# Attention's sums taken two steps at a time, the neighbour mask as a product, and other edits to a two-layer image kernel

## The chip, the cores and the metric

The kernel runs on one core of one Trainium2 chip. Its time is device microseconds of that core. Before the change three runs gave a median of 8884.31 us (8876.86 to 8887.73).

A core has five engines with instruction queues of their own: PE (matrix products; its weight loads are shown as PEld), DVE (vector), ACT (activations and copies), POOL (a second, general vector engine) and SP (used here to issue DMA transfers). Each runs its own queue in order, and they meet only by semaphores.

## The reference

x is two images of 96 channels and 96x96 pixels, float32. Two layers follow each other; each adds a mixing block and then a feed-forward block (FFN).

```python
# layer 0: normalization over channels, then
xz = in_proj(x); xin, z = split(xz)                   # 192 channels each
offset = tanh(conv1x1(gelu(bn(conv3x3(xin)))))        # where to sample
xs = grid_sample(xin, ref + offset)
# 16x16 sub-grids of 36 pixels, 4 directions, 16 states:
h = h * exp(dt * A) + dt * u * B;  y = C . h + D * u  # dt = softplus(dt_w . r + dt_b)
x = x + out_proj(layernorm(sum of 4 directions) * silu(z))
# layer 1: normalization over channels, then
k, v = kv_w . xn;  samp = mean of 2x2 pixels of xn;  q = q_w . samp
attn = softmax over the 9216 keys of (k^T q / sqrt(32))    # 3 heads of 32, 2304 queries
dist = v . attn                                            # 96 x 48 x 48
dmat = softmax over 3x3 neighbours of (xn . samp / sqrt(96))
feature = dmat . (3x3 neighbours of dist)
x = x + proj_w . (feature + depthwise5x5(v) + lepe_b) + proj_b
# both layers: x = x + FFN(normalization(x)), 96 -> 384 -> 96, relu,
# factors rounded to an 8-bit format (5 exponent, 2 mantissa bits), sums to a 16-bit one
```

## The kernel before, in words

**The plan.** Layer 0, and the two outer stages of layer 1, are written as lists of operations, each with an engine, a cost and a due time (`_Plan.op`). `_Plan.order` simulates the engines and their buffers with these costs and takes, engine by engine, the operation that can start first, the due time breaking ties. The order it finds is then held per engine, SP among them. So a changed cost or buffer can move any instruction of the same plan.

**Start.** `_l0_weights` loads layer 0's weights, nearly all on SP's queue, and brings some into other layouts: dt_b (the scan's bias) comes in pieces by 24 tiny loads; A_logs goes by 16 loads into the DRAM tensor `ad` with other strides (L381), is read back as `at` by four loads (L387) and is transposed on PE; `Ds` follows (L400). After these stands the first load of an image's stripe, `xt` (L464).

**Layer 0** (`_layer0`) is one plan over 32 stripes of 576 pixels: a front part (projection, offsets, sampling), the recurrence (`h`, L1045 on DVE and L1050 on POOL), and a back part with the FFN, which writes the result to the DRAM tensor `x2d`. Its buffers lie in four pools, made in the order front, hand, rep, back; the weights' temporaries had the same memory before them.

**Layer 1** (`_layer1`) first loads its weights, builds the neighbour mask (`_l1_mask`) and the FFN's weights, and then does for each image:

1. *Before* (`_l1_before`), a plan over 16 stripes of 576 pixels: load `nxt` from x2d (L1138), normalize (`nxc`, `nva`) into `xn`, which stays in SBUF for the whole image, project `k` (kH) and `v` (vT), pool 2x2 pixels on POOL (xs), project the queries (qH).
2. *Attention* (`_l1_attention`). A bound on the scores is computed and read into a register as a flag; it chooses between a shifted softmax and the plain one, `_l1_packed`, which is what runs. The queries are taken in chunks of 10 rows of 48 (480), the last of 8 rows. A head has 32 channels, so three heads fill three of PE's four row strips; the fourth does in turn a quarter of each head's keys (`SHARED` = 18 blocks of 128). A chunk so has 54 steps in place of 72. A step has four score products of 32 rows (L1382), two exponentials of 960 into `pr` (L1386), four `av` products with the values (L1443), and one DVE addition of all four strips, 1920 elements, into `sums` (L1456), from which the softmax's denominators come. When the fourth strip has done a head, `sums` of it is added to that head's (L1458). PE's order is held: the scores of step j+1 stand before the av products of step j. A chunk ends with `close`, whose parts are run within the next chunk: copy `av` out, products with ones over `sums`, reciprocal on DVE (step 2), products that join the strips, and `dist` = product of both on DVE (step 6).
3. *Rows* (`_l1_rows`), a plan over 8 row blocks of 12 rows: values of the block into `vch` with two edge columns (L1550); per group of 384 pixels the scores with two rows of pooled cells (`st`, L1574), exponential (`e`, L1578), multiplication by the 0/1 mask on POOL (L1580), sums and products with `dist` (`pd`, `po`), feature `ft`; the 25 taps of the depthwise convolution, 20 on DVE as multiply-and-add of 1152 elements (L1612, L1615), five on PE as products with `pt`, the projection scaled by the tap's weight (L1631); the projection of `ft` and of `acc`; then the FFN and the store.

Of the kernel before, what the change touches and what calls it, by code (L numbers as in the profile page):

```python
# [101 lines left out]
class _Plan:  # L102
# [3 lines left out]
    def __init__(self, k):  # L106
        self.k, self.ops, self.slots, self.queues = k, [], {}, {}

# [9 lines left out]
    def op(self, eng, cost, run, r=(), w=(), due=0.0, tab=None, also=()):  # L118
        o = _Op(eng, cost, run, due, tab)
        ref = lambda t: t if isinstance(t, tuple) else (t, None)  # L120
        meets = lambda a, b: a is None or b is None or a == b
        for t, key in map(ref, r):
            o.deps.update(p for p, q in t.writes if meets(key, q))
        for t, key in map(ref, w):
            o.deps.update(p for p, q in t.writes + t.reads if meets(key, q))
        for t, key in map(ref, r):
            t.reads.append((o, key))
        for t, key in map(ref, w):
            t.writes.append((o, key))
        o.deps.discard(o)  # L130
        for t in [x[0] for x in map(ref, list(r) + list(w))] + list(also):
            if t not in o.tiles:
                o.tiles.append(t)
        for t in o.tiles:
            if not t.users and t.tag != "p":
                t.queue.append(t)
            t.users.append(o)
        self.ops.append(o)
        return o
# [127 lines left out]
def _l0_weights(k, a, cp, tmp, ps, dram):  # L267
# [51 lines left out]
    for kg in range(KG):  # L319
        o, kk = kg % 2, kg // 2  # L320
        nc.vector.tensor_copy(k.w_dl[:, :, o, kk * 6 : kk * 6 + 6], xp[:, :, kg, 0:6])
        rows = slice(kk * 6, kk * 6 + 6)
        nc.sync.dma_start(dt_w[rows, o, kk, :], a["dt_w"][kg, :, 0:128])
        nc.sync.dma_start(dt_w[rows, o, 2, kk * 64 : kk * 64 + 64], a["dt_w"][kg, :, 128:])
        b = a["dt_b"]
        for blk in range(2 * NBL):
            half, r = divmod(blk, NBL)
            src = b[r * CB : r * CB + CB, kg, half : half + 1]
            if blk < 4:
                nc.sync.dma_start(k.dt_b[blk::4, o, kk : kk + 1], src)  # L330
            else:
                r0 = kk * 64 + blk - 4
                nc.sync.dma_start(k.dt_b[r0 : kk * 64 + 64 : 2, o, 2:3], src)
        for j in range(4):
            src = xp[:, :, kg, 6 + NS :] if j == 1 else xp[:, :, kg, 6 : 6 + NS]
            nc.vector.tensor_copy(k.w_bc[:, :, o, j, kk, :], src)

# [42 lines left out]
    for n in range(NS):  # L380
        nc.sync.dma_start(ad[n].rearrange("k (d g) -> d k g", g=NG), src[n])  # L381
# [4 lines left out]
    for i in range(NQ):  # L386
        nc.sync.dma_start(  # L387
            at0[i * na : (i + 1) * na], rows[i]
        )
# [10 lines left out]
    nc.sync.dma_start(ds4, a["Ds"])  # L400
# [678 lines left out]
def _layer0(k, tc, a, x, x2d):  # L1079
# [3 lines left out]
    with ExitStack() as st:  # L1083
# [9 lines left out]
        P.front, P.hand, P.rep, P.back = (pool(n, 1) for n in ("front", "hand", "rep", "back"))  # L1093
# [20 lines left out]
        front(0)  # L1114
        for n in range(len(stripes)):
            front(n + 1)
            _l0_scan(k, P, S, n, F[n], tau)
            back(n)
# [7 lines left out]
def _l1_before(k, P, S, W, M, x2d):  # L1126
# [7 lines left out]
    xn, xs, kH, qH, vT, mk, mq = map(held, ("xn", "xs", "kH", "qH", "vT", "mk", "mq"))  # L1134

    def stripe(s):
# [24 lines left out]
        for c in range(2):  # L1161
            norm(c)
        for n, f in enumerate((ALU.max, ALU.min)):
            op("dve", T, lambda n=n, f=f: nc.vector.tensor_reduce(
                mk.ap[:, n, s : s + 1], kH.ap[:C, s * T : (s + 1) * T], AX.X, f),
                ((kH, s),), ((mk, (n, s)),))
# [187 lines left out]
def _l1_packed(k, tc, wk, ps, pa, M):  # L1354
# [3 lines left out]

    nc = k.nc
# [6 lines left out]
    q3 = {}  # L1366
# [7 lines left out]
    def scores(m, j):  # L1374
        n, (p, t) = chunks[m][1] * CELLS, divmod(j, SHARED)
        pr = wk.tile([128, 4, 480], F32, tag="pr", name="pr", bufs=3)
        two = [ps.tile([128, 2, 512], F32, tag="s", name="sc", bufs=3) for _ in range(2)]
        for s in range(4):
            rows = slice(s * HD, (s + 1) * HD)
            k0 = (SHARED + j) * 128 if s < HEADS else (p * SHARED + t) * 128  # L1380
            q = qH[rows, cells(m)] if s < HEADS else q3[m, p][rows, :n]
            nc.tensor.matmul(  # L1382
                two[s // 2][:, s % 2, :n], kH[rows, k0 : k0 + 128], q, start=True, stop=True
            )
        for i in range(2):
            nc.scalar.activation(  # L1386
                pr[:, 2 * i : 2 * i + 2, :n], two[i][:, :, :n], AF.Exp, scale=HD**-0.5
            )
        return pr

    def close(m, av, sums, av3):

        n = chunks[m][1] * CELLS
        avs = wk.tile([128, 480], F32, tag="avs", name="avs", bufs=2)
# [3 lines left out]
        for hd in range(HEADS):  # L1398
            nc.tensor.matmul(
                av[hd * HD : (hd + 1) * HD, :n], k.ones[:, :HD], sums[:, hd, :n],  # L1400
                start=True, stop=True,
            )
# [24 lines left out]
    for m in range(len(chunks)):  # L1427
        n = chunks[m][1] * CELLS
        sums = wk.tile([128, 4, 480], F32, tag="sums", name="sums", bufs=2)
        av3 = wk.tile([128, 2, 480], F32, tag="av3", name="av3", bufs=2)  # L1430
        for j in range(steps):
# [7 lines left out]
            for s in range(4):  # L1439
# [6 lines left out]
                    pr[:, s, :n],  # L1446
# [3 lines left out]
            if j == 0:  # L1450
                nc.vector.tensor_copy(sums[:, :, :n], pr[:, :, :n])
            elif t == 0:
                nc.vector.tensor_tensor(sums[:, :3, :n], sums[:, :3, :n], pr[:, :3, :n], ALU.add)
                nc.vector.tensor_copy(sums[:, 3, :n], pr[:, 3, :n])
            else:
                nc.vector.tensor_tensor(sums[:, :, :n], sums[:, :, :n], pr[:, :, :n], ALU.add)  # L1456
            if t == SHARED - 1:
                nc.vector.tensor_tensor(sums[:, p, :n], sums[:, p, :n], sums[:, 3, :n], ALU.add)  # L1458
                if p < 2:
                    nc.scalar.copy(av3[last, p, :n], other[last, :n])  # L1460
# [3 lines left out]
            if rest and j in (2, 6):  # L1464
                next(rest)
# [52 lines left out]
ON_PE = tuple(range(5))  # L1518


def _l1_rows(k, P, S, W, ffn, M, distT, x2, out, q, at):
# [8 lines left out]
    xn, xs = S.held(M.xn, "xn"), S.held(M.xs, "xs")  # L1530
# [3 lines left out]
    y0 = q * R - 2  # L1534

# [10 lines left out]
    def values(g):  # L1546
# [4 lines left out]
            pv.ap[:C, :n], W.v, xn.ap[:, lo * HW : hi * HW], start=True, stop=True),  # L1551
# [13 lines left out]
    def near(i):  # L1565
        j = 3 * q + i
        toks = slice(j * 384, (j + 1) * 384)
        e = [S.tile(P.wk, [NEAR, 384], "e", 4) for _ in range(2)]
        po, pd, rd = ps("po"), ps("pd"), S.tile(P.wk, [C, 384], "rd", 2)
        for t in range(2):  # L1570
            st = ps("st")

            def part(t=t, st=st):
                op("pe", 384, lambda: nc.tensor.matmul(  # L1574
                    st.ap[:NEAR, :384],
                    xs.ap[:, 2 * j + 2 * t : 2 * j + 2 * t + 2, :].rearrange("p r w -> p (r w)"),
                    xn.ap[:, toks], start=True, stop=True), (xs, xn), (st,), (e[t],))
                op("act", 384, lambda: nc.scalar.activation(  # L1578
                    e[t].ap, st.ap[:NEAR, :384], AF.Exp, scale=C**-0.5), (st,), (e[t],), tab="e")
                op("pool", 384, lambda: nc.gpsimd.tensor_tensor(  # L1580
                    e[t].ap, e[t].ap, W.mask[:, t], ALU.mult), (), (e[t],))
# [26 lines left out]
    for n, t in enumerate(t for t in range(25) if t not in ON_PE):  # L1608
        def tap(n=n, t=t):
# [4 lines left out]
            else:  # L1614
                S.op("dve", 1.6, lambda: nc.vector.scalar_tensor_tensor(  # L1615
# [70 lines left out]
def _l1_mask(k, cp):  # L1686
# [14 lines left out]
    mask = cp.tile([NEAR, 2, 384], F32, tag="mask", name="mask")  # L1701
    m = mask.rearrange("p t (i r w s) -> p t i r w s", i=2, r=2, s=2)
    for t in range(2):
        for i in range(2):
            src = both if t == i else band[:, 1 - t]
            for r in range(2):
                nc.vector.tensor_copy(
                    m[:, t, i, r], src.unsqueeze(2).to_broadcast([NEAR, CELLS, 2])
                )
    return mask  # L1710


def _layer1(k, tc, a, x2d, out):
    nc = k.nc
    with ExitStack() as st:
# [3 lines left out]

        def load(name, shape):  # L1720
            t = cp.tile(shape, F32, tag=name, name=name)
            nc.sync.dma_start(t, a[name])
            return t

        W.k, W.v = load("k_w", [C, C]), load("v_w", [C, C])
        W.q, W.p = load("q_w", [C, C]), load("proj_w", [C, C])
        W.pb, W.lw = load("proj_b", [C, 1]), load("lepe_w", [C, 25])
        W.mask = _l1_mask(k, cp)

        W.pt = cp.tile([C, len(ON_PE), C], F32, tag="pt", name="pt")  # L1730
        for n, t in enumerate(ON_PE):
            nc.vector.tensor_scalar(W.pt[:, n], W.p, W.lw[:, t : t + 1], None, ALU.mult)
        with tc.tile_pool(name="l1t", bufs=1) as tmp, tc.tile_pool(name="l1p", bufs=1, space=PSUM) as ps:
            ffn = _ffn_weights(k, cp, tmp, "f1", a["W1_1"], a["b1_1"], a["W2_1"], a["b2_1"])
            lb = tmp.tile([C, 1], F32, tag="lb", name="lb")
            nc.sync.dma_start(lb, a["lepe_b"])
            pl = ps.tile([128, 512], F32, tag="pl", name="pl")
            nc.tensor.matmul(pl[:C, 0:1], W.p, lb, start=True, stop=True)
            nc.vector.tensor_tensor(W.pb, W.pb, pl[:C, 0:1], ALU.add)
        img = pool("img", 1)  # L1740

        def plan(st, work):
# [3 lines left out]
            S = _Plan(k)  # L1746
            start = len(nc.cur_bb.bb.instructions)
# [4 lines left out]
        for b in range(NB):  # L1752
            M = Ctx()
            M.xn = img.tile([C, NTOK], F32, tag="xn", name="xn")
# [3 lines left out]
            nc.gpsimd.memset(M.dist, 0.0)  # L1758
            with tc.tile_pool(name="kqv", bufs=1) as kqv:
# [5 lines left out]
                with ExitStack() as st:  # L1765
                    plan(st, lambda P, S: _l1_before(k, P, S, W, M, x2d[b]))
                _l1_attention(k, tc, M)
# [13 lines left out]
def tile_metaformer(ctx: ExitStack, tc: tile.TileContext, a, out):  # L1781
# [11 lines left out]

    k.mean96 = filled("mean96", [C, C], 1.0 / C)
# [86 lines left out]
```

## Time and profile before

| what | us |
|---|---|
| median of three runs | 8884.31 |
| the profiled execution | 8876.68 |
| its span, first to last instruction | 8874.9 |
| mean granted PE clock | 0.893 |
| start, before the recurrence | 175.5 |
| layer 0's recurrence | 6565.6 |
| change of layers | 45.5 |
| image 0: before, attention, rows | 78.2, 623.4, 340.8 |
| image 1: before, attention, rows | 81.9, 624.4, 339.6 |

The shares over the whole span are PE 84%, DVE 91%, ACT 72%, POOL 70%; since layer 0 has three quarters of the span, they are mostly layer 0's. The stretches were cut where the first or last instruction of a stage stands in the trace. In the change of layers (6741.1 to 6786.6) PE is busy for 25.7 us and DVE for 7.5.

### The profile page before, as it was taken

The page shows a single profiled execution, that of the slowest core. Times are in us where ns is not written, and L with a number is a line of the kernel's source. Part 1 is how long each engine was busy: PE and PEld are TensorE (multiplying, and loading weights), DVE is VectorE, ACT ScalarE, POOL GpSimd, SP SyncE. Part 2 cuts the span into 40 slices and gives each one's busy share as a digit, 9 for nine tenths or more (in the row PEclk, how much of TensorE's full clock was granted, in tenths as well). Part 3 has the DMA queues.
Part 4 walks back from the last instruction along what each step waited for, and adds up shares of the span by engine and source line. Part 5 has one row for each costly group of instructions (what it writes and reads, how often), then busy time and mean ns, then how long its engine had stood idle before and what let it go on. Part 6 is the DMA issues. An engine that isn't in the chain of part 4 may idle for free. (4 is left out here: it accounts for less than half of the span.)

```text
span 8874.9 us, 120352 instructions
## 1 busy us (share of the span) xinstructions
PE 7426.3 (84%) x43537; PEld 3500.8 (39%) x43537; DVE 8093.4 (91%) x5663; ACT 6381.7 (72%) x10720; POOL 6189.7 (70%) x3931
## 2 busy tenths in 40 slices
PE   6788888888788888888888888888856999989998
PEld 3333334444343344434444433443423333543345
DVE  2999999999999999999999999999996998969988
ACT  4677777777777777777777777777754876677766
POOL 3999999988999889899898889898974001310022
PEclk9899889999988888889898988888956999999999
DMA  2444444444444444444444444444441000010000
GB/s 77 140 143 145 148 142 143 145 142 140 144 142 141 147 142 144 142 146 143 143 142 144 144 139 143 144 140 144 144 131 55 2 2 5 24 28 3 2 10 24
DMA packets 335667, 969.48 MB, mean 109 GB/s; under 512 B 50424, under 2 KB 52144, under 8 KB 334768
## 3 DMA queue, kind: packets, MB, share of 16 engines
q1 hardware_dynamic: 335056, 961.64, 34.2%
q8 instruction: 346, 5.67, 0.3%
q14 instruction: 265, 2.17, 0.1%
HBM read 788.04 MB, written 132.17 MB: 104 GB/s over the span
## 5 line engine op out<-in xcount | busy, mean ns | idle before, releaser
L1050 POOL TENSOR_TENSOR h<-h,cre 128x864 f32<-128x864 f32 x2048 | 4120.9, 2021 | 684.6 <-DVE h L1045 488.5
L1045 DVE TENSOR_TENSOR_SCAN h<-dA,bp 128x864 f32<-128x864 f32 x2048 | 3998.7, 1953 | 83.5 <-PE y L1062 5.4
L1010 ACT ACTIVATE dA<-dlr,A 128x576 f32<-128x576 f32 x3072 | 2156.5, 765 | 1102.2 <-DVE h L1045 1015.6
L1030 DVE TENSOR_TENSOR bp<-dur,B 128x864 f32<-128x864 f32 x2048 | 2173.8, 1061 | 282.2 <-DMA dur<-du_d 42.3
L1062 PE MATMUL y<-h,fold 128*32 128x288 f32 (+2 forms) x18432 | 1870.3, 452 | 167.5 <-POOL h L1050 158.1
L1025 PE MATMUL B<-bt,selb 128*128 128x288 bf16 x2048 | 642.4, 315 | 957.6 <-DVE bp L1030 945.7
L536 PE MATMUL pc<-xin,off 96*96 96x288 f32 x4608 | 1331.0, 416 | 1.0 <-ACT xin L501 0.9
L1062 PEld LDWEIGHTS y<-h,fold 128*32 128x32 f32 x18432 | 762.2, 119 | 1140.4 <-issue 549.6
L1386 ACT ACTIVATE pr<-sc 128x960 f32<-128x960 f32 (+1 forms) x1080 | 955.1, 936 | 255.6 <-DVE sums L1456 144.5
L1456 DVE TENSOR_TENSOR sums<-sums,pr 128x1920 f32<-128x1920 f32 (+1 forms) x510 | 1059.2, 2077 | 58.2 <-ACT pr L1386 7.1
L1537 POOL MEMSET vch<- 96x32 f32 x16 | 2.0, 124 | 1313.8 <-DVE dist L1415 1265.8
L536 PEld LDWEIGHTS pc<-xin,off 96*96 96x96 f32 x4608 | 714.1, 166 | 506.3 <-issue 260.7
L1025 PEld LDWEIGHTS <-selb 128*128 128x128 bf16 x2048 | 200.6, 99 | 1312.3 <-DVE bp L1030 805.8
L1382 PE MATMUL sc<-qH,kH 32*128 32x480 f32 (+1 forms) x3240 | 708.3, 602 | 8.9 <-DMA q<-qH 8.9
L1382 PE MATMUL sc<-q,kH 32*128 32x480 f32 (+1 forms) x1080 | 564.5, 602 | 0.0
L1443 PE MATMUL av<-pr,vT 128*32 128x480 f32 (+1 forms) x4320 | 533.3, 564 | 3.8 <-ACT av L1460 3.5
L1615 DVE SCALAR_TENSOR_TENSOR acc<-vch,lepe_w,acc 96x1152 f32<-96x1152 f32 x304 | 485.7, 1598 | 7.6
L1382 PEld LDWEIGHTS sc<-qH,kH 32*128 32x128 f32 x3240 | 284.5, 184 | 437.5 <-issue 303.0
L709 PE MATMUL pt<-xd,w_dt 96*128 96x288 f32 x768 | 317.7, 507 | 22.9 <-ACT zs L519 10.6
L728 POOL TENSOR_TENSOR e<-e,du 128x576 f32<-128x576 f32 x192 | 271.1, 1412 | 26.6 <-ACT du L724 26.5
L1580 POOL TENSOR_TENSOR e<-e,mask 100x384 f32<-100x384 f32 x96 | 169.0, 1781 | 172.4 <-ACT e L1578 172.1
L730 POOL TENSOR_TENSOR dl<-dl,r 128x576 f32<-128x576 f32 x192 | 270.6, 1410 | 6.2
(260 smaller groups left out, 10113.7 us busy)
## 6 DMA issues: line engine op xcount, KB each, us to landing
cre<-c_d SPq DMA_DIRECT2D x1024, 288.0 KB
dur<-du_d SPq DMA_DIRECT2D x256, 864.0 KB
dlr<-dl_d SPq DMA_DIRECT2D x256, 864.0 KB
x<-xs SPq DMA_DIRECT2D x512, 72.0 KB
du_d<-du SPq DMA_DIRECT2D x128, 288.0 KB
dl_d<-dl SPq DMA_DIRECT2D x128, 288.0 KB
du_d<-du SPq DMA_DIRECT2D x128, 144.0 KB
dl_d<-dl SPq DMA_DIRECT2D x128, 144.0 KB
```

Source lines behind the costliest of these rows:

```text
L536: pe(H2, lambda: nc.tensor.matmul(pc.ap[:C, :H2], k.w_c1[:, ih, tap, oh * C : (oh + 1) * C], xin.ap[:, ih, 3 * c + dy : 3 * c + dy + 3, dx ...
L1010: nc.scalar.activation(dA.ap[:, :, blk, :], dlr.ap[:, blk, :].rearrange("p (c n) -> p c n", c=2), AF.Exp, scale=k.A[:, i, kg, h, blk : blk ...
L1025: nc.tensor.matmul(pB.ap[:, :H2], k.selb[:, kk, i, :], f.bc[o].ap[:, toks], start=True, stop=True)
L1030: nc.vector.tensor_tensor(bp.ap[:, : NBL * H2].rearrange("p (b n) -> p b n", b=NBL), dur.ap[:, :, toks], pB.ap[:, :H2].unsqueeze(1).to_bro ...
L1045: nc.vector.tensor_tensor_scan(hv, dv, bv, 0.0, ALU.mult, ALU.add)
L1050: nc.gpsimd.tensor_tensor(ht.ap, ht.ap, cre.ap[:, toks].unsqueeze(1).to_broadcast([128, NBL, H2]), ALU.mult)
L1062: nc.tensor.matmul(dst, k.fold, v, start=False, stop=stop)
L1382: nc.tensor.matmul(two[s // 2][:, s % 2, :n], kH[rows, k0 : k0 + 128], q, start=True, stop=True)
L1386: nc.scalar.activation(pr[:, 2 * i : 2 * i + 2, :n], two[i][:, :, :n], AF.Exp, scale=HD**-0.5)
L1443: nc.tensor.matmul((main if s < HEADS else other)[s * HD : (s + 1) * HD, :n], vT[:, blk, hd, :], pr[:, s, :n], start=at == 0, stop=at == e ...
L1456: nc.vector.tensor_tensor(sums[:, :, :n], sums[:, :, :n], pr[:, :, :n], ALU.add)
L1615: S.op("dve", 1.6, lambda: nc.vector.scalar_tensor_tensor(acc.ap, src(), W.lw[:, t : t + 1], acc.ap, ALU.mult, ALU.add), (vch,), (acc,))
```

## The change

1. **Layer 0's weights.** dt_w, dt_b, A_logs, `at` and Ds are loaded on ACT's queue instead of SP's. dt_b comes by one load, and products with columns of the identity (`take`, `take2`) put it where it belongs. A_logs goes to `ad` by eight loads instead of 16. Layer 0's pools are made in the order rep, hand, back, front.
2. **Layer 1's weights.** k, q and v weights are loaded during layer 0. All others (`_l1_weights`) follow after image 0's *before*, ahead of its attention. `dist` is cleared there too.
3. **xn.** It is no longer kept: each stripe is stored to the DRAM tensor `xd`, and each row block loads its 16 rows again.
4. **Attention.** `pr` and `sums` hold two steps; one addition of 3840 elements takes both. `sums` has five places per step: for shared heads 0 and 2 the fourth strip stands in front of the others, for head 1 behind them, so that a whole pair stays contiguous in places. Ten ones products in four rounds then add the places up on PE, where three stood; `close` runs in steps 2, 4 and 8. `avs` and `av3` have one buffer each.
5. **Rows.** The mask is no longer a multiplication: a bfloat16 product adds -32768 times the complement of the mask to the scores before the exponential. Four taps are on PE and 21 on DVE. In layer 1's plans PE's costs are multiplied by 0.87, and a tap's cost is 1.43 instead of 1.6.

The diff, cut to its core:

```diff
@@ _Plan.op
-        o = _Op(eng, cost, run, due, tab)
+        o = _Op(eng, cost * self.rate.get(eng, 1.0), run, due, tab)
@@ _l0_weights
-        nc.sync.dma_start(dt_w[rows, o, kk, :], a["dt_w"][kg, :, 0:128])
...
-        for blk in range(2 * NBL):
...
-                nc.sync.dma_start(k.dt_b[blk::4, o, kk : kk + 1], src)
...
+        nc.scalar.dma_start(dt_w[rows, o, kk, :], a["dt_w"][kg, :, 0:128])
...
+    nc.scalar.dma_start(b, a["dt_b"])
...
+    for half in range(2):
+        nc.tensor.matmul(pb[:, 0], take[:, half], b[:, :, half], start=half == 0, stop=half == 1)
...
-    for n in range(NS):
-        nc.sync.dma_start(ad[n].rearrange("k (d g) -> d k g", g=NG), src[n])
+    for d in range(8):
+        nc.scalar.dma_start(dst[:, d], src[:, d])
...
-        nc.sync.dma_start(
+        nc.scalar.dma_start(
             at0[i * na : (i + 1) * na], rows[i]
@@ _layer0
-        P.front, P.hand, P.rep, P.back = (pool(n, 1) for n in ("front", "hand", "rep", "back"))
+        P.rep, P.hand, P.back, P.front = (pool(n, 1) for n in ("rep", "hand", "back", "front"))
...
+        for t, name in zip(k.kvq, ("k_w", "v_w", "q_w")):
+            S.op("sp", 0.2, lambda t=t, name=name: nc.sync.dma_start(t, a[name]), due=64 * tau)
@@ _l1_before
+    xn = S.tile(P.wk, [C, NTOK], "xn", 1)
...
+        S.op("sp", 1.0, lambda: nc.sync.dma_start(
+            M.xd[:, s * T : (s + 1) * T], xn.ap[:, s * T : (s + 1) * T]), ((xn, s),), ())
@@ _l1_packed
+    strips = lambda p: (0, 1, 2, 3) if p % 2 else (1, 2, 3, 0)
+    place = lambda s, p: s if p % 2 else (s + 1) % 4
...
-        pr = wk.tile([128, 4, 480], F32, tag="pr", name="pr", bufs=3)
+        if j % 2 == 0:
+            pairs[m, j] = wk.tile([128, 2, 4, 480], F32, tag="pr", name="pr", bufs=3)
+        pr = pairs[m, j - j % 2][:, j % 2]
...
-        for hd in range(HEADS):
-            nc.tensor.matmul(
-                av[hd * HD : (hd + 1) * HD, :n], k.ones[:, :HD], sums[:, hd, :n],
-                start=True, stop=True,
-            )
+        for r in range(4):
+            for hd in range(HEADS):
+                parts = [sums[:, u, v, :n] for v in ((1,), (2, 4), (3, 0))[hd] for u in range(2)]
+                if r < len(parts):
+                    nc.tensor.matmul(
+                        av[hd * HD : (hd + 1) * HD, :n], k.ones[:, :HD], parts[r],
+                        start=r == 0, stop=r == len(parts) - 1,
+                    )
+            if r == 1:
+                yield
...
-            else:
-                nc.vector.tensor_tensor(sums[:, :, :n], sums[:, :, :n], pr[:, :, :n], ALU.add)
+            if t % 2:
+                pr = pairs.pop((m, j - 1))
+                at = p % 2
+                if j == 1:
+                    nc.vector.tensor_copy(sums[:, :, :4, :n], pr[:, :, :, :n])
+                elif t == 1:
+                    heads = sums[:, :, 1 : 1 + HEADS, :n]
+                    nc.vector.tensor_tensor(heads, heads, pr[:, :, 1 - at : 4 - at, :n], ALU.add)
+                    nc.vector.tensor_copy(sums[:, :, 4 * at, :n], pr[:, :, 3 * at, :n])
+                else:
+                    both = sums[:, :, at : at + 4, :n]
+                    nc.vector.tensor_tensor(both, both, pr[:, :, :, :n], ALU.add)
...
-            if rest and j in (2, 6):
+            if rest and j in (2, 4, 8):
@@ _l1_rows
-ON_PE = tuple(range(5))
+ON_PE = tuple(range(4))
...
+    if q:
+        xn = S.tile(P.wk, [C, R + 4, HW], "xn", 2)
+        S.op("sp", 1.5, lambda: nc.sync.dma_start(
+            xn.ap[:, : min(R + 4, HW - y0)],
+            M.xd.rearrange("p (r w) -> p r w", w=HW)[:, y0 : min(y0 + R + 4, HW)]), (), (xn,))
+    else:
+        xn = S.held(M.xn0, "xn")
...
-                    xn.ap[:, toks], start=True, stop=True), (xs, xn), (st,), (e[t],))
+                        xn.ap[:, toks], start=True, stop=False)
+                    nc.tensor.matmul(
+                        st.ap[:NEAR, :384], W.far, W.mask[:, t], start=False, stop=True)
...
-                op("pool", 384, lambda: nc.gpsimd.tensor_tensor(
-                    e[t].ap, e[t].ap, W.mask[:, t], ALU.mult), (), (e[t],))
...
-                S.op("dve", 1.6, lambda: nc.vector.scalar_tensor_tensor(
+                S.op("dve", 1.43, lambda: nc.vector.scalar_tensor_tensor(
@@ _l1_weights, new, from _layer1
+    W.p = load("proj_w", [C, C])
+    W.pb, W.lw = load("proj_b", [C, 1]), load("lepe_w", [C, 25])
+    W.mask = _l1_mask(k, cp)
+    W.far = cp.tile([NEAR, NEAR], BF, tag="far", name="far")
+    nc.vector.tensor_scalar(W.far, k.ident[:NEAR, :NEAR], -32768.0, None, ALU.mult)
...
+        ffn = _ffn_weights(k, cp, tmp, "f1", a["W1_1"], a["b1_1"], a["W2_1"], a["b2_1"])
...
+    return ffn
@@ _layer1
+            S.rate["pe"] = 0.87
...
+            M.xn0 = img.tile([C, 2 * WIN + 4, HW], F32, tag="xn0", name="xn0")
...
                     plan(st, lambda P, S: _l1_before(k, P, S, W, M, x2d[b]))
+                nc.gpsimd.memset(M.dist, 0.0)
+                ffn = ffn or _l1_weights(k, tc, cp, a, W)
+                nc.sync.dma_start(
+                    M.xn0[:, 2:], M.xd[:, : (2 * WIN + 2) * HW].rearrange("p (r w) -> p r w", w=HW))
                 _l1_attention(k, tc, M)
```

## Prediction

> **What bounds the kernel now.** I read the busy time by stage first, because the page's shares average over stages with different limits.
>
> ```profile
> 0.00:175.50 175.50, 108.03 (x343) 61.38 (x344) 17.34 (x90) 70.09 (x134) 49.31 (x58) 0.88 0.22 62
> 175.50:6741.10 6565.60, 5318.41 (x31328) 2587.54 (x31326) 6247.38 (x4279) 4766.87 (x8186) 5844.08 (x3605) 0.87 0.45 142
> 6864.80:7488.20 623.40, 614.83 (x4400) 191.85 (x4400) 580.51 (x305) 485.00 (x555) 0.00 (x0) 0.98 0.01 2
> 7488.20:7829.00 340.80, 302.38 (x1145) 177.59 (x1145) 288.36 (x248) 219.12 (x470) 117.64 (x84) 0.93 0.07 21
> ```
>
> A line is a stretch, its length, then busy us of PE, PEld, DVE, ACT and POOL, clock, DMA share, GB/s. The second line is layer 0's recurrence (DVE 95%): no edit touches it, and from its first matmul to its last the order of instructions is the same on every engine in both programs. So layer 0 can only be shifted, by what comes before it. The third and fourth lines are image 0's attention and rows stage; image 1 repeats them (624.4 and 339.6 us). Some 1,930 us can change.
>
> In the attention the chain of waits is DVE's additions:
>
> ```profile
> 6877.70 2.17 DVE sums L1456
> 6879.87 0.03 issue
> 6879.90 0.02 DVEq L1456
> 6879.92 0.04 issue
> 6879.97 2.17 DVE sums L1456
> ```
>
> One addition per step, 2.26 us from start to start, of which about 0.1 is the addition's wait for its own predecessor. By shape: 2157 ns for 1920 elements, 1658 for 1440, so 1.04 ns per element and 0.16 us fixed, 0.26 with the wait. But PE is close behind. Where DVE has just lost time and PE, ACT run free, ACT waits for PE:
>
> ```profile
> 7015.75 3.79 ACT L1386 ACTIVATE pr<-sc 128x960 f32<-128x960 f32 x4 [0.30 <-PE sc L1382]
> ...
> 7019.84 3.79 ACT L1386 ACTIVATE pr<-sc 128x960 f32<-128x960 f32 x4 [0.30 <-PE sc L1382]
> ```
>
> Two steps take 4.09 us there: scores, exponentials, av and the scores behind it follow each other at 2.045 us per step. DVE is 10% above that floor.
>
> The start is SP's queue, which issues loads one by one until the first tile of x:
>
> ```profile
> 27.28 10.90 SPq L381 DMA_DIRECT2D ad<-in_A_logs  x16
> 38.22 0.45 SPq L400 DMA_DIRECT2D ds<-in_Ds  x1
> 38.79 1.58 SPq L387 DMA_DIRECT2D at<-ad  x4
> ...
> 44.59 0.31 SPq L464 DMA_DIRECT2D xt<-in_x  x1
> ```
>
> PE's first layer-0 matmul follows at 47.7 us, and nothing overlaps this.
>
> **Start, -25 us.** 24 dt_b loads become one, 16 of A_logs become 8; with dt_w, at and Ds they go to ACT's queue. On SP 17 issues remain up to the first xt (k, q, v among them, 3 x 0.45 us). At 0.45 each, and with nothing landed before about 10 us (ln_b's user starts at 10.12, behind the 1.3 MB off1 load), xt lands at 15 to 18. Changing the pool order frees xt's memory from the weights' temporaries, which it now waits for. What is late next is A: the transpose of `at` stands ahead of xt's matmul on PE. ACT issues 18 DMAs first (some 10 us held up behind off1's landing, then nine at 0.5 to 0.68, the ad row's 630 ns: 16 us), then four at loads by 19, landed 2.9 later as now (38.79 to the copy at 41.71), transposed by 22.3. 47.7 - 22.3 = 25. ACT has nothing else to do then, and DVE's extra copies and PE's four dt_b products (0.2 us each) lie inside that wait. Ends: -15 (ACT issues at 1 us, one landing more) and -33 (xt alone decides).
>
> **Attention, -68 us.** DVE per full chunk of 54 steps now: 51 additions x 2.263 = 115.4; first copy 1.26; twice 1440-addition and copy, 4.2; three 480-additions 2.3; reciprocal and dist 3.6: 126.7, and the reciprocals lie 125.9 us apart. After: one copy of 3840 2.3 (0.52 ns per element by the 1153 and 403 ns copies), 24 additions x (4.0 + 0.263) = 102.3, two split ones 7.7, one 960-addition 1.3, reciprocal and dist 3.6: 117.2. DVE gains 9.6. The Trainium skill (VectorE: DVE Perf Modes, The DRAIN you can't avoid) holds that a semaphore between DVE instructions costs nothing extra. Then some 58 waits now and 28 after fall out of the sums, 120.6 to 114.2, a gain of 6.4. The row decides: the 0.1 us stands in the chain, and 120.6 is not what the reciprocals show.
>
> But PE then has 54 x 2.045 = 110.4, joins 4.6 (7005.96 to 7010.54), and ones products in four rounds in place of one: a round is 0.91 (6996.98 to 6997.89), so 3.6. Sum 118.6 if none overlaps. I take 118.0 between the engines: -7.9 per full chunk, -7 for the short fifth one, -38.6 per image. Against it: the last close runs at half clock (three more rounds x 1.42 = 4.3, less one 0.56 addition), and the first sum waits for two steps (+1): -34 per image. The order of strips leaves each step's eight products as they were: nothing. The single avs and av3 buffers are read by the joins in step 8 of the next chunk, nine steps before av3 is written again: nothing; if not, 1 us per chunk. Ends -30 and -84.
>
> **Rows stage, -24 us.** The mask product leaves POOL:
>
> ```profile
> L1615 DVE SCALAR_TENSOR_TENSOR acc<-vch,lepe_w,acc 96x1152 f32<-96x1152 f32 x304 | 485.7, 1598 | 7.6
> L1580 POOL TENSOR_TENSOR e<-e,mask 100x384 f32<-100x384 f32 x96 | 169.0, 1781 | 172.4 <-ACT e L1578 172.1
> ```
>
> A tap beside an idle POOL takes 1415 ns, beside a mask product 2035. Summed over an image's taps, the excess is 27.3 us beside masks and 6.8 beside POOL's other additions. So DVE loses 27.3 and gets 8 taps x 1.45 = 11.6: -15.7 per image. The Trainium skill (SBUF — State Buffer, SBUF: two separate sides) says that the shared port pair is locked for a whole instruction and the loser is fully blocked: 48 x 1.78 = 85 us per image, five for each one that I count. The row says 0.57 us per product, and I take it. PE: 32 tap products x 0.5 us less (-16), 48 bfloat16 products more at about 0.3 (the 128x288 bfloat16 row is 296 ns): -2 of 275 us that it needs in the same 292. DVE at 276 and PE at 273 are then level, so I take -12. POOL's idle before mask and PE's wait for it (45 us over both images) go too, hidden under the taps. The tail behind the last tap (40 us of projection and FFN) is the same length in both orders. Ends +5 and -20 per image.
>
> **Moved with no net.** xn goes to DRAM by stripe and comes back by row block: 16 stores and 9 loads per image of the size of nxt, which land in 3 us (7829.98 to 7832.94). On SP the nxt loads queue behind a store that waits for DVE, and PE waits for them; three nxt buffers and a 4.8 us stripe cover 3 us. If not, up to +10 per image. Layer 1's weights now delay its first matmul (6779.6 to 6786.6); afterwards the nxt loads, issued at 6744.6 until now, stand behind the last x2d store and land at 6783.4: -3. The FFN weights then stand between the last xn store and the flag: a store's landing, a load's landing and 1.4 us of casts, less the 5 us that the stage's end takes anyway: +3. For q=1 the xn load can start only when attention's memory is free (7488), and its values are wanted at 7500: hidden.
>
> Sum: -25 - 68 - 24 = -117 on 8876.7 (span 8874.9 and 1.8 around it). The median of the runs is 8884.3, the lowest 8876.9; from their middle, 8880, I forecast **8764**.
>
> **Rivals.**
> - PE decides attention (0.17). For: PE shows 99.6% busy, and the reciprocal now stands behind two more rounds. Against: at 2.045 it still keeps up between closes. A chunk of 122: -38 + 8 - 49 = -79, **8802**.
> - DVE alone decides everywhere and only xt the start (0.13): -84 - 32 - 33, **8731**.
> - Pairing does not do what it says, the fixed cost growing with the second dimension of the pair (0.05): +8 - 49, **8839**. Against: 480 to 1920 elements lie on one line.
> - Slower (0.04): with PE nearly gapless in the attention the throttle cuts its clock to the 0.81 of 6000 to 6600 us. PE needs 54 x 1.96 + 8.2 = 114 per chunk; at 0.81, 141: +146 + 8 - 49, **8985**. It decides from a clock of 0.876 down (130 per chunk). Against: attention shows 1.00 today with PE busy throughout, and the low clocks stand where PE idles.
>
> **Numbers.** The forecast has 0.61, its own range 8740 to 8795. The range 8725 to 8808 takes in DVE deciding alone and PE deciding the attention. A measurement tells 0.2% (18 us) from no change: faster 0.95, same 0.01, slower 0.04.
>
> **What would show it.** First layer-0 matmul near 22 us; 3840-element additions of 4.15 us, 4.26 apart; reciprocals 118 apart; taps at 1.42 except beside POOL's additions; attention near 590 and rows near 328 us. Wrong: DVE idle before the additions waiting for ACT, a clock under 1.0 in the attention, PE waiting for nxt before it.

## The result, and the profile after

The changed kernel takes 8781.2 us (median of four runs, 8775.7 to 8785.4) against 8884.9 for the kernel before on the same chip: a ratio of 0.9884 (95% interval 0.9867 to 0.9901), 104 us less. The forecast was 8764, its range 8725 to 8808.

The profiled execution of the changed kernel took 8785.0 us, with a span of 8782.9. Its busy time by stage, in the columns shown before (PE, PEld, DVE, ACT, POOL):

```profile
0.00:153.70 153.70, 110.84 (x352) 63.63 (x353) 17.15 (x98) 70.19 (x134) 49.29 (x58) 0.84 0.25 73
153.70:6730.30 6576.60, 5328.31 (x31327) 2590.71 (x31325) 6247.71 (x4279) 4770.28 (x8186) 5847.41 (x3605) 0.87 0.45 142
6856.30:7450.00 593.70, 584.35 (x4470) 161.30 (x4470) 548.36 (x160) 484.27 (x555) 0.00 (x0) 0.99 0.01 2
7450.00:7780.80 330.80, 296.48 (x1130) 173.36 (x1130) 274.37 (x256) 217.91 (x470) 35.01 (x36) 0.92 0.13 36
```

From the first and last instruction of each stage, in the two kernels and the runs that the argument rests on most (the rows stage here ends at the next stage's first product, or at the last operation of an engine):

| us | before | changed | unpair | start_only | mask_pool | plan_costs | joins_act | best |
|---|---|---|---|---|---|---|---|---|
| first layer-0 product at | 47.7 | 23.2 | 23.1 | 23.1 | 22.9 | 22.9 | 23.1 | 22.7 |
| from there to the first scan step | 127.7 | 130.6 | 127.2 | 128.5 | 132.9 | 129.2 | 128.1 | 127.5 |
| recurrence | 6565.7 | 6576.6 | 6569.6 | 6568.9 | 6562.5 | 6577.2 | 6569.1 | 6570.1 |
| change of layers | 45.4 | 43.0 | 42.2 | 45.5 | 42.4 | 42.6 | 43.7 | 42.8 |
| image 0: before | 78.3 | 83.1 | 83.3 | 78.3 | 83.6 | 80.6 | 82.0 | 81.0 |
| attention | 623.3 | 593.7 | 625.9 | 625.3 | 595.3 | 593.3 | 575.7 | 578.0 |
| rows | 344.8 | 330.8 | 329.8 | 341.9 | 348.3 | 322.5 | 332.6 | 320.3 |
| image 1: before | 78.0 | 79.5 | 79.6 | 78.7 | 78.9 | 79.9 | 80.7 | 79.1 |
| attention | 624.2 | 594.6 | 623.4 | 625.4 | 594.1 | 593.7 | 576.5 | 575.9 |
| rows | 336.6 | 324.5 | 326.5 | 336.4 | 345.5 | 317.8 | 324.0 | 316.3 |

The edited stages of the two profiles differ by -24.5 (start), -2.4 (change of layers), +4.8 and +1.5 (before), -29.6 twice (attention), -14.0 and -12.1 (rows): -105.9 us, close to the medians' -103.7. The two profiles themselves differ by only 92, because the one of before was a short execution of its kernel, that of the changed one a long one of its own, and this lies in layer 0.

The chain of waits in the attention has changed hands. In the changed kernel's lines L1409 are the scores, L1475 the av products, L1429 the ones products, L1439 and L1443 the joins (the products that join the strips), L1493 DVE's additions. At the end of a chunk (start, us, what):

```profile
6975.93 4.17 DVE sums L1493
6980.10 0.04 issue
6980.14 1.81 PE av L1429 x12
6981.95 1.02 PE sc L1409 x8
6982.97 0.94 PE av L1475 x8
6983.91 1.19 PE sc L1409 x8
6985.10 0.94 PE av L1475 x8
6986.04 1.60 PE av L1429 x8
...
6995.83 0.81 PE av L1439 x2
6996.63 0.92 PE av L1443 x2
6997.55 0.92 PE av L1439 x2
6998.47 0.92 PE av L1443 x2
6999.39 0.92 PE av L1439 x2
```

Where one DVE addition followed another, PE's products do: scores and av of two steps take 1.02 + 0.94 + 1.19 + 0.94 = 4.09 us, the pace that the trace of before showed for two steps in which nothing waited for DVE. Between them stand the ones products (L1429, 1.81 and 1.60 us) and the five joins, one after the other (4.49 us). DVE's additions are on the chain only ahead of the ones products, in three of image 0's five chunks: 11.5% of the chain in image 0's attention, where they were 36.0% before. A full chunk takes 119.12 us from reciprocal to reciprocal:

```profile
6990.90 3.15 DVE L1435 RECIPROCAL rden<-av 96x480 f32<-96x480 f32 x1
7110.02 3.15 DVE L1435 RECIPROCAL rden<-av 96x480 f32<-96x480 f32 x1
```

In the groups, the tap is shorter and the mask has left POOL for PE (mean ns of one behind the comma):

```profile
L1666 DVE SCALAR_TENSOR_TENSOR acc<-vch,lepe_w,acc 96x1152 f32<-96x1152 f32 x320 | 469.2, 1466 | 7.9
L1627 PE MATMUL st<-mask,far 100*100 100x384 bf16 x96 | 31.8, 331 | 0.0
```

### The profile page after: what moved, and what is told of

Same layout as the page of the kernel before. It is cut to its first block, busy times and chain, and to the rows that moved or that the text cites. A ratio compares the mean times of both kernels' runs of the same rounds, so it can differ in the third digit from the quotient of the medians.

```text
span 8782.9 us, 119686 instructions
## 1 busy us (share of the span) xinstructions
PE 7366.0 (84%) x43653; PEld 3436.2 (39%) x43653; DVE 8004.4 (91%) x5398; ACT 6381.2 (73%) x10720; POOL 6026.5 (69%) x3835
## 5 line engine op out<-in xcount | busy, mean ns | idle before, releaser
L1493 DVE TENSOR_TENSOR sums<-sums,pr 128x3840 f32<-128x3840 f32 (+1 forms) x240 | 959.1, 3996 | 55.2 <-ACT pr L1413 33.2
L1409 PE MATMUL sc<-qH,kH 32*128 32x480 f32 (+1 forms) x3240 | 627.2, 602 | 9.7 <-issue 4.9
L1409 PE MATMUL sc<-q,kH 32*128 32x480 f32 (+1 forms) x1080 | 564.5, 602 | 0.0
L1475 PE MATMUL av<-pr,vT 128*32 128x480 f32 (+1 forms) x4320 | 532.6, 564 | 3.7 <-ACT av L1500 3.5
L1666 DVE SCALAR_TENSOR_TENSOR acc<-vch,lepe_w,acc 96x1152 f32<-96x1152 f32 x320 | 469.2, 1466 | 7.9
L867 POOL TENSOR_TENSOR x<-x,fy 96x576 f32<-96x576 f32 x32 | 56.1, 1755 | 480.6 <-ACT fy L866 400.6
L1409 PEld LDWEIGHTS sc<-qH,kH 32*128 32x128 f32 x3240 | 219.2, 184 | 418.3 <-issue 218.4
L724 PE MATMUL pt<-xd,w_dt 96*128 96x288 f32 x768 | 313.4, 500 | 26.4 <-ACT zs L534 14.8
```

Source lines behind the costliest of these rows:

```text
L1409: nc.tensor.matmul(two[to // 2][:, to % 2, :n], kH[rows, k0 : k0 + 128], q, start=True, stop=True)
L1475: nc.tensor.matmul((main if s < HEADS else other)[s * HD : (s + 1) * HD, :n], vT[:, blk, hd, :], pr[:, place(s, p), :n], start=at == 0, st ...
L1493: nc.vector.tensor_tensor(both, both, pr[:, :, :, :n], ALU.add)
L1666: S.op("dve", 1.43, lambda: nc.vector.scalar_tensor_tensor(acc.ap, src(), W.lw[:, t : t + 1], acc.ap, ALU.mult, ALU.add), (vch,), (acc,))
```

## The experiments

Each run starts from the kernel before or the changed one; lines and stages as above. Single runs of one kernel differ by up to 16 us in all (seven runs of the kernel before: 8874.4 to 8890.8), so small differences are read from the stages.

**Attention undone (unpair).** The function `_l1_packed` of before in the changed kernel.

```diff
-            pairs[m, j] = wk.tile([128, 2, 4, 480], F32, tag="pr", name="pr", bufs=3)
+        pr = wk.tile([128, 4, 480], F32, tag="pr", name="pr", bufs=3)
...
-                    both = sums[:, :, at : at + 4, :n]
-                    nc.vector.tensor_tensor(both, both, pr[:, :, :, :n], ALU.add)
+                nc.vector.tensor_tensor(sums[:, :, :n], sums[:, :, :n], pr[:, :, :n], ALU.add)
```

> The changed kernel with the attention of before (one addition per step, three ones products, order of strips and buffers as before); start, weights, xn's way and rows stay changed. If the additions were what attention's time came from, a full chunk goes back from 119.1 to 125.9 us, each attention from 594 to 624 us, and the whole to about 8781 + 60 = 8841. Rival: part of attention's gain comes from elsewhere (memory free of xn, other loads, weights): then attention stays below 615 us.

Measured 8839.6 us (four runs), ratio to before 0.9956 (0.9939 to 0.9972). Reciprocals stand 125.9 to 126.3 us apart again and the attention takes 625.9 and 623.4. Attention's whole gain, 29 to 32 us per image, comes from the edits of this function taken together (pairing, order of strips, buffers); the other parts of the change give 40 us.

**The start alone (start_only, queue_only).** In the kernel before:

```diff
@@ _l0_weights as changed; start_only also:
-        P.front, P.hand, P.rep, P.back = (pool(n, 1) for n in ("front", "hand", "rep", "back"))
+        P.rep, P.hand, P.back, P.front = (pool(n, 1) for n in ("rep", "hand", "back", "front"))
```

> The kernel before with only the start's edits (loads on the other queue, dt_b by products, eight loads of A_logs, order of the pools). Theory: first layer-0 product at 23 us, first scan step 22 us earlier than before (the 24.5 won, less 3 given back on the way to the first scan step), and no change after: 8884.9 - 22 = 8863. Rival: layer 0's recurrence, 11 us longer in the changed kernel's profile with the same order of instructions, is really longer with the new place of its buffers: then it is 6576 us here too and about 8874 results.

> The kernel before with the start's loads moved and merged, but with layer 0's pools in their old order, so that xt's memory was the weights' temporaries'. Theory: the first xt load waits until the last of these is read (the copies and the transposition end at about 22 us) and lands 2.5 us later: first layer-0 product at 25 to 30 us instead of 23. Rival: the order of pools does nothing: 23 us.

start_only: 8857.6 us (12 runs), ratio 0.9977 (0.9968 to 0.9985), 22.4 less than the 8880.0 beside it. First product at 23.1 us, recurrence 6568.9: the rival, a longer layer 0, falls. queue_only (one run, 8863.7): first product at 26.4. There SP's queue shows that the pools' order is the other 3.3 us; the load of x waits behind xr until the temporaries are read, whose last reader on PE, the transposition of `at`, ends at 22.6:

```profile
16.00 0.42 SPq L881 DMA_DIRECT2D xr<-in_x  x1
23.10 0.31 SPq L478 DMA_DIRECT2D xt<-in_x  x1
```

In the changed kernel that load is issued at 18.69 and is no longer what comes last. The transposition of `at` is, as the PE timeline shows:

```profile
22.39 0.39 PE L407 MATMUL pa<-ident,at 96*128 96x96 f32 x1 [7.59 <-DVE Dsum L418]
23.17 2.85 PE L490 MATMUL axc<-xt,less_mean 96*96 96x384 f32 x4 [0.39 <-ACT A L410]
```

It waits for DVE's copy of `at` (L405), and this copy for DVE's own queue. The waits for the four loads were over at 20.4 us, but DVE had been busy without a gap since 14.9, and the copy had its turn at 21.98:

```profile
L405 DVEq EVENT_SEMAPHORE  x2: 21/36/50, 20.3 to 20.4; - x2
18.69 2.60 DVE L373 CAST selb<-ident 32x128 bf16<-32x128 f32 x16
21.98 0.27 DVE L405 COPY at<-at 96x128 f32<-96x128 f32 x1
```

So up to 1.6 us of the start are now DVE's order of operations; no run moves the copy ahead.

**Who decides the attention now (half_sums).** DVE's paired additions take two of four places; half of the denominators' terms are left out.

```diff
-                    both = sums[:, :, at : at + 4, :n]
-                    nc.vector.tensor_tensor(both, both, pr[:, :, :, :n], ALU.add)
+                    both = sums[:, :, at : at + 2, :n]
+                    nc.vector.tensor_tensor(both, both, pr[:, :, 0:2, :n], ALU.add)
```

> The changed kernel, whose paired additions take only two of the four places of a pair (1920 of 3840 elements; half of the denominators' terms are left out). This takes about 2 us from each of 24 additions, some 47 us of DVE per chunk. Theory: PE now decides attention (54 steps of 2.046, two double rounds of ones products 3.4, joins 4.6: 118.4), so that nothing changes: reciprocals 119 us apart, attention 593 us. Rival: DVE (117.2 by its own sum) still decides for a part: then the distance falls to 118.4 or below and the attention to 590 or less.

The stretch of image 0's attention:

```profile
6847.10:7435.80 588.70, 582.55 (x4470) 163.02 (x4470) 318.77 (x160) 484.19 (x555) 0.00 (x0) 0.99 0.01 2
```

DVE has 230 us less to do in it (318.8 for 548.4), and the five reciprocals span 449.1 us, as without this edit (448.7 and 450.3). So over whole chunks DVE no longer decides anything: PE's waits for its additions within the chunks are gone, and yet a full chunk takes 119.45 us, 0.3 more (why was not looked into). The attention as a whole is still 5 us shorter, below the 590 that I had given the rival: 2 us before the first reciprocal and 3.3 behind the last one. These 3.3 us are not additions saved. The last five joins ran at a granted clock of 0.50 in the changed kernel and of 1.00 here, 7.15 us for 3.87 (the first line is the changed kernel's):

```profile
7442.20:7449.40 7.20, 7.15 (x10) 0.90 (x10) 0.00 (x0) 0.00 (x0) 0.00 (x0) 0.50 0.00 0
7431.30:7435.30 4.00, 3.87 (x10) 0.68 (x10) 0.04 (x2) 0.00 (x0) 0.00 (x0) 1.00 0.00 0
```

The whole took 8759.9 (one run); what this is below 8781 beyond the 10 us of the two attentions lies in stages that the edit doesn't touch.

**PE's part of the close (joins, joins_act).** In the changed kernel, the three joins first, then the two products that add the fourth strip; in joins_act also the reciprocal on ACT.

```diff
@@ close
         for hd in range(HEADS):
             rows = slice(hd * HD, (hd + 1) * HD)
             nc.tensor.matmul(av[rows, :n], k.join[:, rows], avs[:, :n], ...)
-            if hd < HEADS - 1:
-                nc.tensor.matmul(av[rows, :n], k.ident[last, last], av3[last, hd, :n], ...)
+        for hd in range(HEADS - 1):
+            rows = slice(hd * HD, (hd + 1) * HD)
+            nc.tensor.matmul(av[rows, :n], k.ident[last, last], av3[last, hd, :n], ...)
@@ joins_act
-        nc.vector.reciprocal(rden[:, :n], av[:C, :n])
+        nc.scalar.activation(rden[:, :n], av[:C, :n], AF.Ln)
+        nc.scalar.activation(rden[:, :n], rden[:, :n], AF.Exp, scale=-1.0)
```

> The changed kernel with the order of the joins' products changed: the three 128x32 products first, then the two 32x32 ones that add to them (before, one of each in turn; in the trace they follow each other at 0.92 us). If the three overlap as the ones products do (0.9 us for three) and the two do as well, PE has 2.7 us less per chunk: 116.4. Theory: DVE (117.2) decides then: reciprocals 117.2 to 117.6 us apart, attention 585 to 587 us, the whole 12 to 16 us shorter. Rival, PE alone: 116.4, attention 581, the whole 25 us shorter. If the order doesn't let them overlap: no change.

> The same, and the reciprocal (3.03 us on DVE) taken as exp of minus ln on ACT, two instructions of about 0.5 us. DVE has 114.1 us per chunk then and PE 116.4. Theory: PE decides at 116.4 to 117, attention about 580 us with a shorter last chunk, the whole 27 to 33 us below the changed kernel, about 8750. Rival: the two instructions stand ahead of exponentials that PE waits for, about 1 us per chunk: 117.4, the whole 15 to 20 us shorter.

joins: 8746.8 us (four runs), ratio 0.9851 (0.9835 to 0.9868), 34 below the changed kernel's median; the two attentions give 28 of it. Its chain of waits at the same place:

```profile
6984.46 0.94 PE av L1476 x8
6985.40 0.81 PE av L1439 x6
6986.21 0.92 PE av L1444 x4
6987.13 1.02 PE sc L1409 x8
```

Five joins take 1.73 us where they took 4.49. Reciprocals stand 116.7 us apart, attention is 579.9 and 580.8: the rival's numbers (PE alone, 116.4 and 581), not mine, which had DVE hold the chunk at 117.2. My sum for DVE was too long by at least 0.5 us. The two engines are level now: DVE's additions are 36% of the chain in image 0's attention again. joins_act: 8742.4 us (four runs), ratio 0.9843 (0.9826 to 0.9859). A full chunk is 0.25 us shorter (116.45 between the `dist` operations, 116.71 in joins), and each attention 4 us, 3 of it in the last close. There the granted clock was 1.00, in joins 0.64 during the ones products (2.78 us for 4.29), so that a part of the 4 us is the clock and not the reciprocal; in best, with the same edit, image 0's last ones products took 4.32 again. In all 39 us below the changed kernel's median, more than my 27 to 33; 36 of it stand in the two attentions. The rival's price for the two ACT instructions doesn't show.

**The mask on POOL again (mask_pool).** In the changed kernel:

```diff
-                    nc.tensor.matmul(
-                        st.ap[:NEAR, :384], W.far, W.mask[:, t], start=False, stop=True)
...
+                op("pool", 384, lambda: nc.gpsimd.tensor_tensor(
+                    e[t].ap, e[t].ap, W.mask[:, t], ALU.mult), (), (e[t],))
```

> The changed kernel with the mask again as POOL's multiplication after the exponential, without the bfloat16 product; 21 taps stay on DVE. Theory: a product on POOL costs the taps 0.57 us each, 27 us per image, and DVE paces the stage: DVE's busy time in the rows stage goes from 274 to about 301 us and the stage from 331 and 328 to about 350 and 347. Rival: PE paces the stage (296 of 331 us busy): then POOL's slowing is hidden and the stage moves by under 8 us. If the shared port were locked for a whole product, the excess would be 85 us per image and the stage near 390.

8812.1 us in one run. Rows 348.3 and 345.5 us, DVE's busy time in image 0's 299.0 us in place of 274.4. Groups of mask_pool, DVE and POOL:

```profile
L1666 DVE SCALAR_TENSOR_TENSOR acc<-vch,lepe_w,acc 96x1152 f32<-96x1152 f32 x320 | 519.4, 1623 | 8.6 <-ACT vch L1601 0.4
L1631 POOL TENSOR_TENSOR e<-e,mask 100x384 f32<-100x384 f32 x96 | 169.3, 1781 | 247.2 <-ACT e L1629 225.3 <-PE fxc L812 21.7
```

The same 320 taps cost 519.4 - 469.2 = 50.2 us more with 96 products of 1.78 us on POOL: 0.52 us per product, not 1.78. The mask's move is worth 17.5 and 21.0 us per image: the last tap ends 21.4 and 24.3 us later here, but what the plan leaves behind it is 3.9 and 3.4 us shorter.

**Four or five taps (five_taps).** `ON_PE = tuple(range(5))` in the changed kernel.

> The changed kernel with five taps on PE and 20 on DVE, as before. Theory: the two engines were level, so that eight taps less on DVE (-11.6 us) and 32 products more on PE (+16 us) per image move the rows stage by +2 to +8 us. Rival: DVE paces it, and the stage gets 8 to 12 us shorter.

Rows 332.0 and 328.4 us, 1.2 and 3.9 longer (8786.1 in one run); DVE busy 263.7, PE 303.3 in image 0's. The rival's gain of 8 to 12 us is not there. Whether it is longer at all, as expected, is near what two profiles can tell: other runs with the changed kernel's rows stage took 326.4 to 332.6 and 322.2 to 327.0.

**The plan's costs (plan_costs).** In the changed kernel:

```diff
-            S.rate["pe"] = 0.87
+            S.rate["pe"] = 1.0
...
-                S.op("dve", 1.43, ...
+                S.op("dve", 1.6, ...
```

> The changed kernel with the plan's costs as before (PE's not multiplied by 0.87, a tap 1.6). Only the order of instructions in layer 1's outer stages differs. Theory: the rows stage is set by DVE's and PE's sums, and either order comes close: 331 and 328 us move by less than 3. Rival: part of the rows stage's gain is the order: 5 us or more longer per image.

Rows 322.5 and 317.8 us, 8.3 and 6.7 shorter, and outside the range just given; 8765.3 us in one run although its layer 0 was the longest of all. Neither of my expectations came: I had the stage move by less than 3 us, or, by the rival, get longer without the new costs. Here the change had lost time. Where, shows image 1's rows stage cut at its last tap. Changed kernel:

```profile
8454.90:8741.70 286.80, 273.04 (x1050) 160.37 (x1051) 269.98 (x246) 188.73 (x409) 24.67 (x31) 0.96 0.14 36
8741.70:8782.90 41.20, 22.14 (x81) 12.30 (x79) 4.43 (x10) 28.95 (x62) 4.91 (x4) 0.67 0.07 22
```

plan_costs:

```profile
8442.00:8729.80 287.80, 276.39 (x1072) 164.50 (x1073) 270.43 (x248) 191.79 (x415) 26.63 (x31) 0.97 0.13 37
8729.80:8763.30 33.50, 14.45 (x57) 8.30 (x56) 4.01 (x9) 26.31 (x55) 3.80 (x3) 0.67 0.07 20
```

The taps end after 287 us in both. But with the changed costs the plan leaves 81 products behind the last tap instead of 57, 22 us instead of 14. ACT, which has the FFN to do, waits for them, and has 2.6 us more of its own left (28.95 for 26.31): the chain of the changed kernel has taps on PE there, and ACT's timeline the wait.

```profile
8745.71 1.95 PE pp L1682 x8
8747.66 0.48 PE pp L1686 x2
8748.14 0.50 PE fxc L812 x2
```

```profile
8748.67 0.41 ACT L817 ACTIVATE fsq<-fxc 96x288 f32<-96x288 f32 x1 [3.15 <-PE fxc L812]
```

Which of the two costs does it was not tried.

**Where the weights and xn go (weights_early, keep_xn).**

```diff
@@ weights_early: the changed kernel with
+                ffn = ffn or _l1_weights(k, tc, cp, a, W)
                 with ExitStack() as st:
                     plan(st, lambda P, S: _l1_before(k, P, S, W, M, x2d[b]))
-                ffn = ffn or _l1_weights(k, tc, cp, a, W)
@@ keep_xn: unpair with
-        S.op("sp", 1.0, lambda: nc.sync.dma_start(M.xd[:, s * T : (s + 1) * T], ...
...
+            M.xn = img.tile([C, NTOK], F32, tag="xn", name="xn")
```

> The changed kernel with the remaining weights of layer 1 loaded and built ahead of image 0's first stage, as before, instead of behind it. Theory: the change of layers goes from 43 to about 46 to 50 us and image 0's first stage from 83 to about 79, so that the whole moves by less than 5 us. Rival: the move was worth more: change of layers over 52.

> The changed kernel with the attention of before and with xn kept in memory for the whole image, as before: no stores to DRAM, no loads back. To be read against the changed kernel with the attention of before alone. Theory: the stores and loads are hidden, so that the stages of image 1 (79.6 and 326.5 us) and image 0's rows (329.8) agree within 2 us. Rival: stores hold up the nxt loads: image 1's first stage 5 to 10 us shorter here.

weights_early: change of layers 45.9, image 0's first stage 79.8 (43.0 and 83.1): the same sum to 0.4 us, 8781.0 in one run. keep_xn: first stages 79.6 and 78.4, rows 328.9 and 322.8, against unpair's 83.3, 79.6, 329.8 and 326.5. The stores and loads are not quite hidden, some 9 us in the profiles, 6.5 between 8833.2 (one run) and unpair's median. Of these 3.7 us are in image 0's first stage; the rows stages lie within what profiles with the same rows stage show.

**Both finds together (best).** joins_act with the plan's costs of before.

> The changed kernel with the joins' new order, the reciprocal on ACT, and the plan's costs as before (PE's not multiplied, a tap 1.6): the two finds together. They lie in different stages and should add: attention 576 us, rows stage about 323 and 318, the whole about 8742 - 15 = 8727. Rival: the shorter rows stage was one run's chance: then it stays at 8742 and the rows stages near 331 and 325.

8719.3 us (five runs, 8714.5 to 8726.5), ratio to before 0.9818 (0.9805 to 0.9831), some 60 us below the changed kernel. Attention 578.0 and 575.9, rows 320.3 and 316.3: they add. Image 0's last ones products at the lower clock (above) are most of the difference between the two attentions.

## Why the prediction was right, point by point

- **Start, -25.** Right in size, and in what came last: the transposition of `at`, at 22.39 us (22.3 stated), with the first product at 23.17; start_only gained 22.4 us as a whole. That it came within 0.1 us of the stated time was luck. The loads had landed by 20.4, 1.5 us before the sum had them (19 and 2.9), and DVE's queue, which I had inside that wait, held the copy until 21.98. Two to three us less than counted lie between first product and first scan step, a stretch that took 126 to 133 us in the runs.
- **Layer 0 shifted only.** Right. In the profiles of 14 kernels (the two and the twelve runs), which share layer 0's order of instructions, the recurrence took from 6562.5 to 6577.2 us, start_only's 6568.9 among them; the changed kernel's 6576.6 is such a run, not a cost.
- **Attention, -34 per image.** Measured -29.6. The step that is off is the chunk: I took 118.0 as a compromise between DVE (117.2) and PE (118.6), and it is 119.1. PE decides. My sum for it, which I took as a ceiling, was right to 0.2 (110.4 + 3.4 + 4.6 = 118.4 measured); to it come two delays per chunk behind ACT's copies of the fourth strip's `av`, a wait of 0.36 ahead of the av products after 18 steps and some 0.4 after 36, where the scores wait for an exponential behind such a copy (1.49 us for 1.0 to 1.2), and in two of image 0's five chunks a wait of 0.5 and 1.0 for DVE's last addition ahead of the ones.

```profile
7058.11 1.49 PE sc L1409 x6
DVE sums L1456 <- ACT pr L1386: 3.3, 2, 2.3
DVE sums L1493 <- ACT pr L1413: 16.4, 10, 4.3
```

The last two lines (us in total, times, longest) show one of my own signs of being wrong: DVE waits for ACT ahead of the additions, 16.4 us in image 0's attention for 3.3 before. So the rival "PE decides attention" was right in its mechanism, at a chunk of 119.1 and not of its 122. Half_sums shows that less work for DVE does not shorten the chunks taken together, and joins that DVE's own limit lies at 116.7 or lower.
- **The additions.** Right by the row, not by the sentence. Two of them stand in the changed kernel's DVE timeline as 8.42 us with 4.16 of work each, so 4.26 apart as counted. The Trainium skill (VectorE: DVE Perf Modes, The DRAIN you can't avoid) has a semaphore between DVE instructions cost nothing extra. In this trace each addition has a semaphore instruction of its own before it (240 for 240) and starts 0.10 us behind the end of the one before; most taps have none (4 for 320) and start 0.03 us behind.
- **Rows, -12 per image.** Measured -14.0 and -12.1. The last tap ends 13.2 and 11.6 us earlier within the stage than before (287.7 for 300.9, 286.8 for 298.4), and the tail behind it stayed as long as it was, as stated. DVE's busy time fell by 14.0 (15.7 counted). 5.6 of the 14.0 are the first taps of the eight blocks, multiplications with one tensor input; they took 0.81 us alone and up to 3.52 beside POOL's instructions. Before and after:

```profile
L1612 DVE TENSOR_SCALAR acc<-vch,lepe_w 96x1152 f32<-96x1152 f32 x8 | 12.1, 1514 | 9.6 <-ACT vch L1553 9.4
L1663 DVE TENSOR_SCALAR acc<-vch,lepe_w 96x1152 f32<-96x1152 f32 x8 | 6.5, 809 | 7.3 <-ACT vch L1601 7.3
```

The counted loss had them in it. For the multiply-and-add taps alone, the mask's price of 0.57 us per product was close: 0.52 (the 85 us against it are three for each one that I count, not five); by the Trainium skill's full lock (SBUF — State Buffer, SBUF: two separate sides) mask_pool would have been near 390 us and was 348. What the prediction didn't see is that the tail was not a given: with the plan's costs of before it is 8 us shorter, and the stage would have gained 22 and 19.
- **No net from what moved.** Right to a few us: -3 at the change of layers (measured -2.4), +3 for the weights ahead of the flag (+4.8, of which the stores of xn have a part: without them image 0's first stage is 3.7 shorter), the move of the weights itself 0.4. That the stores and loads of xn cost nothing is the part that was a little too good.
- **The sum.** -25 - 68 - 24 = -117 against -103.7: 9 of the 13 are the attention's chunk.

## What to carry to other kernels

When an engine 10% above the next one was relieved here, the next one's own sum with its waits was the answer, not a value between the two: write down every product that the change adds to it, and look first at those that run one by one. The joins overlapped only where those of one shape and of different column groups stood together; their order alone was worth 28 us in the two attentions. A planner's costs are an edit like any other: look at what they leave behind the last instruction of the engine that bounds the stage, not only at that engine's sum.

## What the runs showed of the hardware

- Three products of 128x32 and 480 columns to three column groups took 0.81 us together, and two of 32x32 0.92; in turn, writing to the same group in pairs, each of the five took 0.8 to 0.9. The order changed both the sequence of groups and that of shapes (128 rows, 32 rows), so which of the two costs the time stays open.
- A POOL product of 1.78 us slows DVE's multiply-and-add taps beside it by 0.52 us on average, far less than its own length; a first tap of a block, with one tensor input, took up to 3.52 us for 0.81.
- The last joins of an attention took 7.15 us at a granted clock of 0.50 (changed kernel) and 3.87 at 1.00 (half_sums).
- With identical order of instructions, layer 0's 6570 us varied by 15 us from execution to execution: more than several of the edits are worth, so these could be read only from their own stages.
